# Cross attention and routing of a decoder kernel: another written order, and parts of norms, copies and query scalings exchanged between VectorE and ScalarE

## The chip, the core and the metric

The kernel runs on one core of a Trainium2 chip, which has a tensor engine (TensorE, PE in the profile), a vector engine (VectorE, DVE), a scalar engine (ScalarE, ACT), GpSimd (POOL), and SyncE (SP), whose queue issues most of the DMAs. Each engine works through its own list of instructions in order and waits on semaphores for the others. The metric is the device time of one execution in microseconds.

## The reference

Two decoder layers over x of shape (2, 1024, 256), each step added to x: a linear attention with a feed-forward part, a cross attention to latents, a recurrent cell; then a causal attention, a cross attention to 64 rows of text, and a mixture of experts. The change lies in the last two:

```python
x = x + _L1_attn_ref(_layernorm(x), ...)
x = x + _L1_xattn_ref(_layernorm(x), ctx_768, ...)
x = x + _L1_ffn_ref(_layernorm(x), ...)

# _L1_xattn_ref: 16 heads of 16 channels, 64 keys
q = (x @ wq + bq); k = (y @ wk + bk); v = (y @ wv + bv)
attn = softmax(q k^T / sqrt(16)); out = (attn @ v) @ wo + bo

# _L1_ffn_ref: 8 groups of 256 tokens, 8 experts, room for 64 tokens of a group in each
logits = x @ router_w
dispatch, combine = _gating_top2(softmax(logits), C)   # best two experts, places by running count
hidden = gelu(expert_inputs @ w0) * (expert_inputs @ w1)
expert_outputs = hidden @ wo
```

_layernorm subtracts the mean of a row and divides by the square root of its variance plus 1e-5.

## The kernel before

All 2048 tokens stay in SBUF as `x`, 128 tokens to a tile, 16 tiles. Cross attention and routing go by *units* u = 0 to 3 of four tiles (512 tokens). The class `Cross` has one method for each step of a unit, `Experts` has the routing, and the order of all of it is a text written by hand: `CROSS_ORDER` (L1633), which `Cross.run` reads word by word (L2010). A word names a step, the digit(s) after it the unit and the half, chunk or pair. `FIRST_ORDER` (L2024) does the same for the routing of unit 3 beside the first half of the first expert (L2336). No scheduler moves instructions inside these texts: each engine gets its instructions in this order, and semaphores do the rest.

The steps of a unit in cross attention, with the engine that runs each:

| step | engine | work |
|---|---|---|
| `stat`, `mean` | VectorE | row statistics (L1797), mean and variance (L1803), EPS added (L1804) |
| `root` | POOL | power -1/2 (L144) |
| `norm` | VectorE | (x - mean) x r for two tiles, `ln_apply` (L183) |
| `bias` | POOL | output bias added to x once it is normalised (L204) |
| `turn`, `xT` | TensorE, ScalarE | transposes (L1825), copy from PSUM (L1829) |
| `proj`, `q` | TensorE, both | query projection; + bias and x 0.25: chunk 0 on VectorE (L1846), chunk 1 on ScalarE (L1848) |
| `max`, `red` | TensorE, VectorE | scores once (L1856), row maxima (L1867) |
| `part` | VectorE | the maxima split into three bf16 parts: casts and subtractions (L1878, L1880) |
| `mT`, `rows` | TensorE, ScalarE | maxima transposed (L1890) and copied (L1894) |
| `sc`, `exp` | TensorE, ScalarE | transposed scores minus maxima (L1903), exponentials (L1915) |
| `val`, `os` | TensorE, ScalarE | values (L1922), copy (L1932) |
| `sum`, `inv`, `spr`, `yT` | TensorE, VectorE | sums (L1940), reciprocal (L1949), spread (L1959), product (L1971) |
| `out`, `add` | TensorE, VectorE | output projection (L1979), added to x (L1989) |

`text`, `vals` and `keys` prepare keys and values of a batch entry b (units 0 and 1 use b = 0, units 2 and 3 b = 1). The statistics of units 0 and 1 are taken early, beside the end of the causal attention (`Cross.stats`, L1722).

Routing of unit u is the generator `Experts.scores`, of which each word `route_...` runs the next piece: `stat` (L2126), `mean` (L2130, L2131), `root`, `norm`, `turn` (L2143), `xT` (L2146), `prod` (L2151, the product with the router's weights), `copy` (L2159). `choose` runs one of eight pieces of the top-2 choice of a batch entry, `ones` builds a tile's one-hot places (L2239, L2240), `disp` multiplies tokens by them (L2250, dispatch), `put` copies the result (L2258). `up` is the pair of first products of a chunk of the hidden layer (L2407), eight matmuls of 256 columns in `FIRST_ORDER`; `gelu` (L2418) and `mul` (L2422) follow on ScalarE and VectorE. There are eleven chunks, `00` to `0a`.

PSUM tiles of two banks come from a ring called `s`: three slots in the cross attention stage (`banks("ps_f", 3, 2, 0)`), two with the experts (`banks("ps_c", 2, 2, 2)`). A step that takes a slot waits for the last reader of what lay there.

## Time and profile before

Three runs: 1716.50, 1719.92 and 1722.71 us, median 1719.92. The profile is of one execution more, of 1725.12 us, whose instructions span 1723.4 us.

| stretch, us from the span's start | length | PE busy | DVE busy | ACT busy | POOL busy | granted clock |
|---|---|---|---|---|---|---|
| up to the end of the causal attention, 0 to 1121.6 | 1121.6 | 1064.31 | 612.18 | 412.34 | 216.51 | 0.97 |
| cross attention, routing, start of the experts, 1121.6 to 1268 | 146.4 | 132.72 | 94.81 | 45.75 | 15.54 | 0.92 |
| experts, 1268 to 1723 | 455.0 | 450.55 | 97.03 | 64.42 | 87.55 | 1.00 |

A row of instructions in the profile gives the start and length in us, the engine, the line, the operation, what it writes and reads, and in brackets how long the engine stood idle before it and what it waited for. A length runs from an instruction's start to its end; instructions of one engine that follow one another overlap a little, so four norms of 0.406 us take 1.37 together. In the chain of waits each row is a piece of time on the chain of work that ended last. The granted clock is TensorE's, as a share of its full speed.

### The profile page before, as it was taken

Reading aid. Unit: us, or ns where it says so; the run is one execution under the profiler, and the core shown is the slowest. Engines: PE = TensorE matmul, PEld = TensorE weight load, DVE = VectorE, ACT = ScalarE, POOL = GpSimd, SP = SyncE. Lnnn points to the kernel's source line nnn. Section 1 sums busy time; section 2 is a strip of 40 time slices with the busy share of each in tenths; the row PEclk is TensorE's granted clock in tenths of the full one; section 3 lists DMA queues with packets and bytes.
Section 4 is the critical chain, followed back from the end, with each engine's and each line's share of the span. In section 5 each row is a group of like instructions: output and inputs, shape, how many; then the busy total and the mean of one; then the engine's idle time right before and its main releaser. Section 6 shows DMA issues by size and latency. Waiting matters only on the chain.

```text
span 1723.4 us, 21309 instructions
## 1 busy us (share of the span) xinstructions
PE 1647.6 (96%) x8815; PEld 885.6 (51%) x8822; DVE 804.0 (47%) x1454; ACT 522.5 (30%) x876; POOL 319.6 (19%) x376
## 2 busy tenths in 40 slices
PE   7998899999999999999999999989999999999998
PEld 5746454343433447443433443446785664666466
DVE  8514236646654425476676668376531311111322
ACT  2321231432223323235455455423221111111110
POOL 2001140342222301113111011220035000000520
PEclk9999999999999999979999999989899999999999
DMA  5000000000000100100000000080014322232321
GB/s 232 1 1 3 1 0 0 1 1 1 1 1 1 40 1 1 32 1 2 1 2 1 1 1 1 2 273 2 1 68 164 122 84 66 95 122 72 106 64 49
DMA packets 36824, 69.68 MB, mean 40 GB/s; under 512 B 5048, under 2 KB 28152, under 8 KB 36344
## 3 DMA queue, kind: packets, MB, share of 16 engines
q1 hardware_dynamic: 28712, 53.61, 9.3%
q0 software_dynamic: 4608, 11.54, 2.1%
q10 hardware_dynamic: 3408, 3.17, 0.5%
q8 instruction: 70, 1.15, 0.3%
q14 instruction: 26, 0.21, 0.0%
HBM read 54.15 MB, written 14.16 MB: 40 GB/s over the span
## 4 chain that ended last, share of the span: by engine, by line
PE 80%; DVE 11%; issue 5%; ACT 2%; POOL 1%; DMA 0%; ACTq 0%; POOLq 0%; DVEq 0%
PE ps_s L2407 18%; PE ps_o L2434 9%; PE ps_s L1396 8%; PE ps_o L1436 5%; PE ps_s L1020 4%; PE ps_t L1355 4%; PE ps_o L947 3%; PE ps_t L1201 3%; PE ps_t L1471 2%; PE ps_s L908 2%; PE ps_t L539 2%; PE ps_s L822 2%; PE ps_s L381 2%; DVE part L915 1%; PE ps_f L556 1%
## 5 line engine op out<-in xcount | busy, mean ns | idle before, releaser
L2407 PE MATMUL ps_s<-xe,w 128*128 128x512 f32 (+1 forms) x528 | 229.0, 592 | 0.0
L1506 ACT ACTIVATE pT<-ps_t 128x512 f32<-128x512 f32 (+3 forms) x344 | 150.6, 490 | 150.3 <-PE ps_t L1471 148.9
L1396 PE MATMUL ps_s<-kT,qT 32*128 32x512 f32 (+3 forms) x768 | 182.9, 574 | 10.0 <-DVE part L1412 6.2
L1471 PE MATMUL ps_t<-qT,kT 32*128 32x512 f32 (+3 forms) x688 | 185.6, 557 | 2.2 <-ACT pT L1506 2.2
L2422 DVE TENSOR_TENSOR hid<-ga,ps_s 128x512 f32<-128x512 f32 (+2 forms) x99 | 62.0, 628 | 266.4 <-ACT ga L2418 266.3
L2407 PEld LDWEIGHTS ps_s<-xe,w 128*128 128x128 f32 (+1 forms) x528 | 98.0, 187 | 121.3 <-issue 120.0
L2434 PE MATMUL ps_o<-wo,hid 128*128 128x256 f32 (+1 forms) x704 | 153.7, 379 | 0.0
L1412 DVE TENSOR_REDUCE part<-ps_s 128x2 f32<-128x1024 f32 (+3 forms) x128 | 130.6, 1024 | 46.9 <-PE ps_t L1471 38.8
L2434 PEld LDWEIGHTS ps_o<-wo,hid 128*128 128x128 f32 (+1 forms) x704 | 133.2, 190 | 18.6 <-issue 0.5
L2418 ACT ACTIVATE ga<-ps_s 128x512 f32<-128x512 f32 (+2 forms) x99 | 54.4, 550 | 245.3 <-PE ps_s L2407 244.0
L1464 POOL TENSOR_SCALAR_AFFINE_SELECT pT<-pT 128x256 f32<-128x256 f32 x128 | 52.2, 408 | 319.5 <-ACT pT L1506 311.7
L1396 PEld LDWEIGHTS ps_s<-kT,qT 32*128 32x128 f32 x768 | 61.6, 195 | 86.8 <-issue 45.2
L1436 PE MATMUL ps_o<-pT,vr 128*32 128x256 f32 (+4 forms) x1408 | 99.3, 360 | 1.8 <-POOL pT L1464 1.5
L1027 ACT ACTIVATE pT<-ps_s 128x1024 f32<-128x1024 f32 x64 | 65.5, 1024 | 115.6 <-PE ps_s L1020 115.6
L915 DVE TENSOR_REDUCE part<-ps_s 128x2 f32<-128x1024 f32 x64 | 76.4, 1218 | 28.4 <-PE ps_s L908 27.7
L1032 POOL TENSOR_TENSOR acc<-acc,pT 128x1024 f32<-128x1024 f32 x24 | 59.5, 2480 | 152.7 <-ACT pT L1027 148.1
L1404 DVE TENSOR_TENSOR ps_s<-ps_s,causal 128x256 f32<-128x256 f32 x128 | 55.0, 430 | 66.6 <-PE ps_t L1471 44.6
L2407 PE MATMUL ps_s<-xin,w 128*128 128x256 f32 (+3 forms) x264 | 81.7, 471 | 0.5 <-DVE hid L2422 0.5
L1436 PEld LDWEIGHTS ps_o<-pT,vr 128*32 128x32 f32 x1408 | 29.0, 109 | 99.3 <-issue 85.4
L1471 PEld LDWEIGHTS ps_t<-qT,kT 32*128 32x128 f32 x688 | 71.6, 192 | 12.1 <-ACT pT L1506 6.9
L908 PE MATMUL ps_s<-kT,qT 64*128 64x512 f32 x256 | 71.5, 639 | 0.8 <-DVE part L898 0.6
L1020 PE MATMUL ps_s<-qT,kT 64*128 64x512 f32 x256 | 70.2, 625 | 0.2 <-DVE part L915 0.2
(401 smaller groups left out, 2361.8 us busy)
## 6 DMA issues: line engine op xcount, KB each, us to landing
w<-in_w SPq DMA_DIRECT2D x32, 684.0 KB, 8.5
wo<-in_wo SPq DMA_DIRECT2D x8, 1280.0 KB, 7.0
xi_rows<-xin SPq DMA_DIRECT2D x8, 384.0 KB, 8.1
eo_rows<-rows ACTq DMA_DIRECT2D x12, 256.0 KB, 5.5
xr<-xi_rows POOLq DMA_DIRECT2D x48, 64.0 KB, 7.3
w_ffn<-in_w_ffn SPq DMA_DIRECT2D x1, 2304.0 KB, 13.9
x<-in_x SPq DMA_DIRECT2D x4, 512.0 KB, 5.4
w<-in_w_cell SPq DMA_DIRECT2D x2, 1024.0 KB, 16.5
```

Source lines behind the costliest of these rows:

```text
L908: nc.tensor.matmul(s3[:, hh, :], lhsT=q[rows, qt * P : (qt + 1) * P], rhs=kt[rows, half * 512 : (half + 1) * 512], start=True, stop=True,)
L915: nc.vector.tensor_reduce(part[:, half, qt, :], s3, AX.X, ALU.max, negate=True)
L1020: nc.tensor.matmul(s3[:, hh, :], lhsT=self.ones_h[hr, :] if i else kt[hr, kk * P : (kk + 1) * P], rhs=rows[hr, cols] if i else q[hr, cols] ...
L1027: nc.scalar.activation(pT, s3, AF.Exp)
L1355: nc.tensor.matmul(s, lhsT=self.w[name][:, kc, grp * P : (grp + 1) * P], rhs=self.xT[b][:, kc, cols], start=(kc == 0), stop=(kc == DC - 1),)
L1396: nc.tensor.matmul(s3[:, hh, :n], lhsT=q[rows, qt * P : (qt + 1) * P], rhs=kt[rows, at : at + n], start=True, stop=True,)
L1412: nc.vector.tensor_reduce(out, s3[:, :, :n], AX.X, ALU.max, negate=True)
L1436: nc.tensor.matmul(self.o[hh * 32 : hh * 32 + 32, cols], lhsT=vr[:, kk, 4 * grp + hh, :], rhs=pts[hh // 2][:, hh % 2, cols], start=first, ...
L1471: nc.tensor.matmul(out, lhsT=kt[rows, kk * P : (kk + 1) * P], rhs=q[rows, j * 512 + q0 : (j + 1) * 512], start=True, stop=True,)
L1506: nc.scalar.activation(pT[:, hh, q0:], heads[hh][:, q0:], AF.Exp)
L2407: self.k.nc.tensor.matmul(s[:m, i * 512 : i * 512 + n], lhsT=wt[:, kc, at : at + m], rhs=self.inputs[e][:, kc, first : first + n], start=( ...
L2434: self.k.nc.tensor.matmul(o, lhsT=self.hid[:n, hc, st * P : (st + 1) * P], rhs=self.to[:n, hc, :], start=(hc == 0), stop=(hc == len(HCH) - 1),
```

## The change

A quote mark behind a word of an order (`norm_11'`) now sets `k.other` for that step. Norm steps with it run on ScalarE, as x r + shift with shift = -mean x r, a new small step (`shift`) of each unit on VectorE. Copies with it (`xT`, `rows`, `os`, `route_xT`, `route_copy`, `put`) run on VectorE. `q` with it swaps which engine scales. The words of both orders stand in another sequence: unit 1 goes ahead of unit 0, and the routing, choice and expert steps interleave differently. Six of eight norm steps are marked in the cross attention, six of eight in the routing.

```diff
+    def copy(self, out, in_, act=True):
+        if act != self.other:
+            self.nc.scalar.copy(out, in_)
+        else:
+            self.nc.vector.tensor_copy(out, in_)
...
+    def normed(self, out, in_, mv, r, shift, i):
+        if self.other:
+            self.nc.scalar.activation(
+                out, in_, AF.Identity, bias=shift[:, i : i + 1], scale=r[:, i : i + 1]
+            )
+        else:
+            self.ln_apply(out, in_, mv, r, i)
+
+    def shifted(self, shift, mv, r):
+        self.nc.vector.scalar_tensor_tensor(shift, mv[:, :, 0], -1.0, r, ALU.mult, ALU.mult)
...
 CROSS_ORDER = """
-text_0 stat_31 norm_00 norm_01 stat_30 turn_00 bias_0 turn_01 vals_0 text_1 keys_0 xT_0 stat_20 proj_00
-vals_1 keys_1 proj_01 norm_11 stat_21 q_00 q_01 norm_10 max_01 mean_3 bias_1 mean_2 turn_11 red_010
-turn_10 xT_1 red_011 root_2 proj_11 root_3 norm_21 norm_20 max_00 norm_30 bias_2 norm_31 proj_10 red_001
-bias_3 red_000 q_11 q_10 part_0 max_10 turn_30 red_100 turn_31 xT_3 turn_20 red_101 turn_21 max_11 xT_2
-mT_0 red_110 rows_0 red_111 sc_00 part_1 exp_00 mT_1 rows_1 sc_01 proj_21 exp_01 proj_20 sc_10 q_20 q_21
-val_0 exp_10 max_20 os_0 sum_0 red_200 red_201 sc_11 inv_0 proj_30 exp_11 proj_31 max_21 q_30 q_31 sum_1
-red_210 red_211 spr_0 inv_1 val_1 yT_0 part_2 os_1 out_0 spr_1 add_0 mT_2 route_stat_01 rows_2 yT_1
-route_stat_00 max_30 route_mean_0 route_root_0 out_1 red_300 route_norm_01 route_norm_00 red_301
-route_turn_0 add_1 route_xT_0 route_stat_10 max_31 route_stat_11 red_311 route_prod_0 route_mean_1
-red_310 route_root_1 route_copy_0 route_norm_11 sc_20 route_norm_10 part_3 route_turn_1 exp_20 mT_3
-route_xT_1 sc_21 rows_3 route_prod_1 exp_21 route_copy_1 sc_31 choose_0 choose_0 sum_2 exp_31 choose_0
-choose_0 inv_2 spr_2 choose_0 val_2 choose_0 os_2 yT_2 choose_0 sc_30 choose_0 out_2 exp_30 ones_03
-ones_02 ones_01 ones_00 disp_00 add_2 route_stat_20 sum_3 put_00 ones_07 ones_06 ones_05 val_3 inv_3
-ones_04 spr_3 os_3 route_stat_21 disp_01 yT_3 route_mean_2 put_01 out_3 route_root_2 route_norm_20
-route_norm_21 add_3 route_turn_2 route_xT_2 route_prod_2 route_copy_2
+text_1 norm_10 norm_11' stat_30 norm_01' bias_1 stat_20 turn_11 vals_1 turn_10 keys_1 text_0 xT_1
+norm_00 bias_0 proj_10 vals_0 keys_0 proj_11 stat_21 mean_2 turn_01 root_2 q_11' q_10' turn_00 stat_31
+max_10 xT_0 mean_3 shift_2 root_3 proj_01 norm_20' red_100 norm_21' red_101 proj_00 bias_2 shift_3
+norm_31' max_11 q_00 q_01 norm_30' turn_20 red_110 turn_21 bias_3 xT_2 red_111 turn_31 turn_30 part_1
+max_00 xT_3 red_000 mT_1 rows_1 red_001 max_01 red_010 red_011 sc_11 part_0 exp_11 mT_0 rows_0 sc_10
+proj_20 exp_10 proj_21 sc_00 q_21 q_20 val_1 exp_00 max_20 os_1' sum_1 red_200 red_201 sc_01 inv_1
+proj_31 exp_01 proj_30 max_21 q_31' q_30' sum_0 red_210 red_211 spr_1 inv_0 val_0 yT_1 part_2 os_0 spr_0
+out_1 yT_0 mT_2 add_1 max_31 rows_2 route_stat_11 out_0 route_stat_10 route_mean_1 red_311 route_root_1
+route_shift_1 red_310 route_norm_10' route_norm_11' add_0 sc_21 route_stat_01 route_turn_1 exp_21
+route_stat_00 route_mean_0 route_xT_1' route_root_0 max_30 route_shift_0 route_norm_00' route_prod_1
+red_301 route_norm_01' red_300 route_turn_0 part_3 sc_20 route_xT_0 route_copy_1' mT_3 exp_20
+route_prod_0 rows_3' sc_30 route_copy_0 choose_0 sum_2 exp_30 val_2 inv_2 choose_0 choose_0 spr_2 os_2
+choose_0 yT_2 choose_0 choose_0 sc_31 choose_0 out_2 exp_31 choose_0 ones_03 ones_01 ones_02 sum_3 add_2
+route_stat_20 val_3 inv_3 ones_00 route_stat_21 spr_3 os_3 route_mean_2 disp_00 yT_3 route_root_2
+route_shift_2 route_norm_21 route_norm_20' out_3 ones_06 put_00 ones_07 ones_05 ones_04 route_turn_2
+add_3 disp_01 route_xT_2 route_prod_2 put_01 route_copy_2
 """
...
 FIRST_ORDER = """
-up_06 route_stat_30 up_08 gelu_06 route_stat_31 route_mean_3 mul_06 route_root_3 gelu_08 mul_08 up_04
-route_norm_30 route_norm_31 route_turn_3 gelu_04 mul_04 route_xT_3 route_prod_3 up_01 route_copy_3
-choose_1 choose_1 choose_1 gelu_01 choose_1 up_00 choose_1 mul_01 choose_1 gelu_00 mul_00 up_0a choose_1
-choose_1 up_05 gelu_0a ones_12 ones_13 up_07 gelu_05 ones_10 ones_11 mul_0a gelu_07 disp_10 mul_07
-mul_05 up_02 put_10 ones_15 ones_16 ones_14 up_09 gelu_02 ones_17 mul_02 disp_11 gelu_09 mul_09 up_03
-put_11 gelu_03 mul_03
+route_stat_30 route_stat_31 route_mean_3 route_root_3 route_shift_3 up_09 route_norm_30 route_norm_31'
+route_turn_3 gelu_09 up_07 route_xT_3' mul_09 route_prod_3 gelu_07 mul_07 up_0a route_copy_3' choose_1
+choose_1 up_06 gelu_0a choose_1 choose_1 choose_1 gelu_06 mul_0a mul_06 up_08 choose_1 choose_1 up_03
+gelu_08 mul_08 choose_1 up_02 gelu_03 ones_13 ones_10 up_01 ones_11 gelu_02 ones_12 mul_03 disp_10
+gelu_01 mul_02 mul_01 up_04 put_10 ones_15 ones_16 ones_14 up_05 gelu_04 ones_17 mul_04 disp_11 gelu_05
+mul_05 up_00 put_11' gelu_00 mul_00
 """
...
+    def shift(self, u):
+        mv, r, sh = self.early[u]
+        self.k.shifted(sh, mv, r)
...
-        if c == 0:
-            k.nc.vector.tensor_scalar(q[:, 0, :], s[:, :512], k.vec("xq_b", 0), 0.25, ALU.add, ALU.mult)
+        s = s[:, c * 512 : (c + 1) * 512]
+        if (c == 0) != k.other:
+            k.nc.vector.tensor_scalar(q[:, c, :], s, k.vec("xq_b", c), 0.25, ALU.add, ALU.mult)
         else:
-            k.nc.scalar.activation(q[:, 1, :], s[:, 512:], AF.Identity, bias=self.qb[:, 1:2], scale=0.25)
+            k.nc.scalar.activation(q[:, c, :], s, AF.Identity, bias=self.qb[:, c : c + 1], scale=0.25)
...
         for step in CROSS_ORDER.split():
-            name, args = step.rsplit("_", 1)
+            k.other = step.endswith("'")
+            name, args = step.rstrip("'").rsplit("_", 1)
```

## The prediction

> **What bounds the kernel now.** I read the page's busy shares and slices first, then the busy time by stage, then the chain of waits inside the stage that the change rewrites, then single instructions there.

> ```profile
> PE 1647.6 (96%) x8815; PEld 885.6 (51%) x8822; DVE 804.0 (47%) x1454; ACT 522.5 (30%) x876; POOL 319.6 (19%) x376
> PE   7998899999999999999999999989999999999998
> PEclk9999999999999999979999999989899999999999
> ...
> 1121.60:1268.00 146.40, 132.72 (x1202) 93.62 (x1201) 94.81 (x254) 45.75 (x63) 15.54 (x10) 0.92 0.25 81
> 1268.00:1723.00 455.00, 450.55 (x1506) 277.08 (x1504) 97.03 (x191) 64.42 (x112) 87.55 (x112) 1.00 0.30 96
> ```

> The first number after each stretch is its length, the next is TensorE's busy time, and the one before the DMA share is the granted clock. TensorE bounds the whole (96%), and nearly all of what comes after 1268 us (450.55 of 455.00). The rewritten stage is 1121.6 to 1268 us: 13.7 us without a matmul (146.40 - 132.72), and a clock of 0.92. Only these two can be won, since the number of matmuls doesn't change.

> ```profile
> 1130.00:1140.00 10.00, 6.71 (x46) 3.86 (x44) 9.93 (x25) 1.70 (x2) 5.20 (x4) 0.69 1.01 386
> 1140.00:1150.00 10.00, 8.07 (x118) 5.40 (x116) 8.88 (x13) 2.58 (x3) 3.94 (x2) 0.97 0.92 244
> ...
> 1190.00:1200.00 10.00, 8.52 (x83) 5.63 (x85) 8.01 (x21) 5.04 (x6) 1.01 (x1) 0.93 0.01 2
> ...
> 1230.00:1240.00 10.00, 8.90 (x37) 7.53 (x35) 4.89 (x19) 2.87 (x4) 1.01 (x1) 0.66 0.01 2
> ```

> Where TensorE waits most, VectorE (third pair of numbers) is full: 9.93 of 10 us, while ScalarE works 1.70. The chain of waits runs almost wholly over VectorE from 1122.0 to 1147.9 us, and again from 1182.0 to 1198.3. Part of it, and the same time on POOL:

> ```profile
> 1132.91 2.13 DVE ve L1804
> 1135.67 2.01 POOL rs_y L144 x2
> 1137.70 4.70 DVE xh L183 x8
> 1142.40 2.27 DVE m L1867 x2
> ...
> 1132.66 2.35 POOL L204 TENSOR_TENSOR x<-x,rows 128x1024 f32<-128x1024 f32 x1 [5.39 <-DVE xh L183]
> 1139.15 2.45 POOL L204 TENSOR_TENSOR x<-x,rows 128x1024 f32<-128x1024 f32 x1 [1.48 <-DVE xh L183]
> ```

> The add of EPS to 128x4 numbers (L1804) takes 2.13 us here and 0.17 us the next time; eight norms take 4.70 us where four take 1.37. Both overrun while a bias add runs on POOL, and end as it ends: 4.0 us lost (2.13 - 0.17, and 4.70 - 8 x 0.34).

> **The change, part by part.** Durations below are pitches where instructions follow one another: a norm 0.345 us on VectorE (1.37 / 4), 0.50 on ScalarE (the three norms of L1311 at 671.9 us take 1.58, one alone 0.59), a statistics pair 0.66, keys 1.41, values 0.46, one max reduction 1.135, the three-way split `part` 1.5.

> *Up to the end of the second split (before: 1122.46 to 1154.25 us, 31.8).* VectorE's work is memset 0.48, eight statistics 2.65, sixteen norms 5.5, values 0.92, keys 2.82, means 1.05, two query scalings 1.4, eight reductions 9.1, two splits 3.0: 26.9, with 4.0 blocked and 0.9 waiting. Six of the eight norm steps are primed and leave VectorE (12 x 0.345 = -4.1); two `shift` come (+0.3). ScalarE takes them in idle time (12 x 0.5 = 6.0 in a stretch where it works 1 to 3 us in 10). The query scalings only swap sides: whichever comes second waits for the first, as before (the ScalarE one starts at 1131.97, when VectorE's ends). The blocked 4.0 go: placing the steps in their new order at these pitches, bias_1 runs 1123.8 to 1126.2 and bias_0 1127.6 to 1130.0, beside statistics, keys and values, which ran at normal pace beside a bias add before (1124.9 to 1127.3), and bias_2 lies beside work that reads PSUM. But bias_3 now waits for the late norm_30' on ScalarE (about 1139.4) and runs to 1141.9, over part_1, due at 1140.3. Before, both splits ran after the last bias add. What that costs the rows don't show: nothing, or all 1.6 us. [...] By the row alone (only single-input norms and the EPS add were seen blocked) it may be 0[...]. I take 1.6. Waits for TensorE: 1.0 for q_00 behind two projections, 1.2 for max_10 and max_11. End: 1122.46 + 26.9 - 4.1 + 0.3 + 1.6 + 2.2 = 1149.4, 4.8 earlier.

> From there to the end of max_20 TensorE took 11.7 us before (to 1165.92). Now mT 0.6, scores 1.3, proj 3.6, scores 1.3, val 1.9 with a 0.2 wait, max 1.1 = 10.0. That would be 6.4 us gained; but 1.5 of it is full clock where the rows of before are slow (mT 1.01 and scores 2.41 at 1154), and TensorE again stands about 2 us ahead of mT_0, so I take the same slow rows: **-5.0** (between -6.4 and -1.5, the latter if the projections of unit 0 also run at half clock: 8 x 0.43 = 3.4 on q_00's path).

> *Second stretch (1177.07 to 1204.93).* From yT to the end of part_3 VectorE loses eight norms (-2.76), gains the copy xT_1 (a PSUM copy of that size is 1.22 on VectorE, L444, 1.01 on ScalarE) and two shifts (+0.24): -1.3, with 0.2 less waiting, -1.5. Behind part_3 lay mT_3, scores, route product, scores (6.66, two of them slow); now one score step stands ahead of mT_3 and 4.6 remain: -2.1. os_1 and rows_3 as VectorE copies (1.22, and 0.69 after the bf16 copy L935) fall where VectorE waited 2 to 6 us. Sum -3.5; less 0.8 for half clock, which low activity may bring here as before (0.93): **-2.7** (-3.5 to -0.5).

> *Third stretch, to the end of route product 2 (1204.93 to 1234.32).* The matmuls alone are 25.5. Before, TensorE waited 1.07 for the copy os_2 and 1.10 for xT_2, and the product ran 2.67 instead of 2.05. Now val_2 stands ahead of the choose steps (1.8 us of TensorE work over a 1.01 copy), and disp_01 (1.8) between turn_2 and product 2: **-2.8** (-3.5 to -1). If the cover were gone, the two copies would be back at 2.2.

> *First expert half (1234.32 to 1267.45, 33.1).* Group 3's statistics can't begin before product 2 ends, since they reuse the closed pool's memory (VectorE waited 3.48 for it before). Chain: statistics 1.4, mean 0.9, root 1.0, shift and hand-overs 0.5, ScalarE's norms 1.1 = 4.7 us. Before, three ups (24 matmuls) covered it; now one does, at 1.78: TensorE idles 2.9. Then up_07 is a third user of two PSUM slots: up_09 holds one until mul_09, turn_3 the other until xT_3', both queued on VectorE, mul_09 behind the copy (and gelu_09 behind norm_31' and a 1.28 table load): 1.5 more. Behind up_07 wait product 3 and the choice, and the scatter behind that. After such idling I expect half clock for about 3.4 us. [...] while the row 1230:1240 shows 0.66 after waits of 1.1. [...] by the row 3.5, 1.4, 2.7. I take the row. Sum: 1.8 + 2.9 + 1.4 + 1.5 + 3.5 + 2.7, then eight ups 14.2, choice 1.8, dispatch 3.6, small waits 0.6 = 34.0: **+0.9** (-1.7 to +3).

> *Without effect:* two shifts in the attention before (0.17 each where VectorE idles 2 to 7 us); put_11', copy_1', copy_3' (under 0.5 each, beside ups). No moved step issues a DMA and SP's queue keeps its order; POOL only gets its bias adds and roots at other times. After 1268 us TensorE is full and everything moves up as one.

> **Sum.** -5.0 - 2.7 - 2.8 + 0.9 = -9.6. The profiled execution: span 1723.4 to 1713.8, its time 1725.1 to 1715.5. The median before, 1719.9, is 5.2 below that execution; the same step gives 1710.3.

> **Rivals.** (1) *The clock eats the gain.* Each microsecond of matmuls at half clock costs 0.5. If the first stretch (-1.5), the second (-0.5) and the expert start (+1) come near their bad ends and the third holds: -3.8, so 1716.1. For it: 0.69, 0.93 and 0.66 all follow short waits. Against: turn_01 and turn_00 now fill the gap ahead of max_10. (2) *Everything fits:* full clock after mT_0 and in the expert start, part_1 not blocked: 1.5 + 1.6 + 0.8 + 2.5 more, 1704. Against: four bad ends must all fail. (3) *Slower:* the expert start stays at half clock. One up costs 1.78 more; the gain of 10.5 up to there is used up after six ups, and if all eight later ups and the dispatches run so, (14.2 + 3.6) - 10.5 + 0.9 = +8, 1728. For it: 1230 to 1250 us had about 10 us at half clock. Against: in a run of ups the clock was back at 1.00 by 1250. (4) *The gain is given back later,* where weights arrive for the experts: those of the first two are in by 1150, later loads follow the slots they reuse, and TensorE waits 4.5 us in 455, so this only adds to (1).

> **How the numbers follow.** My forecast has 0.62 (1705.5 to 1715), rival 1 with 4 has 0.20, rival 2 has 0.12, rival 3 has 0.06. 0.3% of this time is 5.2 us, about what a measurement can tell from no change: the bounds are 1714.7 and 1725.1. Faster: 0.58 + 0.12 + 0.05 = 0.75; same 0.04 + 0.15 = 0.19; slower 0.06. The range reaches from rival 2, less 1, to the near side of no change: 1703 to 1718.5.

> **What would show it.** L1804 at 0.17 us and no run of norms above its pitch; part_1's first cast near 1.9 us under bias_3; the second split ending near 1149.4; max_20 ending near 1161, the fourth score step near 1197, product 2 near 1224, the second dispatch of the first half near 1258. TensorE's waits of 2.9 and 1.5 us around turn_3, the second for xT_3' or mul_09. Wrong would be: VectorE no longer full up to the second split with ScalarE's norms late instead; a clock under 0.9 over 1121 to 1260; or a step of before that I held fixed moving by itself.

## The result, and the profile after

The changed kernel took 1719.64 us (median of 12 runs, 1707.97 to 1723.59). The kernel before, timed again beside it, took 1724.45 (12 runs, 1716.50 to 1726.71). The medians lie 4.8 us apart. The ratio on record is 0.9963, 95% interval 0.9945 to 0.9982, which makes it 6.4 us. Two later comparisons gave 0.9964 (0.9945 to 0.9983; e8) and 0.9964 (0.9948 to 0.9981; e15), again with medians only 4.9 and 4.6 apart, so the gain is known as some 5 to 6 us. The forecast was 1710.3 with a range of 1703 to 1718.5, so the direction was right and the size wrong: 9.6 us were forecast, and 1719.64 lies above the range.

The profiled execution of the changed kernel took 1708.17 us with a span of 1706.4. That is 17.0 us less than the profiled execution before, and most of it has nothing to do with the change. The last add of the layer before, which ends the unchanged part, starts at 1121.99 us before and at 1111.34 after (one row of each profile):

```profile
1121.99 0.42 DVE L1549 TENSOR_TENSOR x<-x,ps_t 128x256 f32<-128x256 f32 x1 [1.45 <-PE ps_t L1544]
1111.34 0.42 DVE L1569 TENSOR_TENSOR x<-x,ps_t 128x256 f32<-128x256 f32 x1 [1.44 <-PE ps_t L1564]
```

These 10.65 us lie in code that is the same in both but for two shift steps of 0.16 us. The stretch view shows where some of it comes from (columns as in the prediction; the clock is the third number from the end). Before, then after:

```profile
720.00:760.00 40.00, 35.53 (x181) 16.12 (x179) 26.51 (x40) 9.58 (x21) 3.68 (x9) 0.62 0.00 1
150.00:200.00 50.00, 39.37 (x121) 22.61 (x120) 24.37 (x72) 12.58 (x22) 12.54 (x20) 0.90 0.00 0
```

```profile
720.00:760.00 40.00, 36.10 (x252) 16.46 (x254) 30.73 (x44) 12.63 (x33) 6.25 (x16) 0.79 0.00 1
150.00:200.00 50.00, 39.36 (x135) 22.01 (x134) 24.77 (x72) 14.04 (x24) 12.19 (x17) 1.00 0.00 1
```

The granted clock differs in equal code, 0.62 against 0.79. A later profile of the changed kernel (e15) has the 0.62 and 0.90 of before, and its last add at 1122.04. So the clock's course differed between executions of one kernel (0.79 and 0.62 over the same 40 us), and the two profiles may be compared only inside the stage, with times counted from that last add. The page after, and the stage with what follows:

```profile
PE 1631.9 (96%) x8815; PEld 879.0 (52%) x8822; DVE 801.7 (47%) x1446; ACT 529.2 (31%) x892; POOL 319.3 (19%) x376
...
PEclk9999999999999999989999999999899999999999
```

```profile
1111.10:1249.50 138.40, 127.13 (x1194) 91.42 (x1194) 91.24 (x242) 51.73 (x78) 15.50 (x10) 0.94 0.26 85
1249.50:1706.00 456.50, 452.00 (x1513) 278.39 (x1511) 97.86 (x193) 64.26 (x111) 87.36 (x112) 1.00 0.30 96
```

The stage takes 138.4 us where it took 146.4; of these 8.0, 0.87 are four output products that lay in the stage before and lie behind it now (the rest is 456.5 against 455.0 us). VectorE is busy 3.6 us less and ScalarE 6.0 more, as the marks say.

Two details of the first stretch. VectorE and POOL in the timeline:

```profile
1124.04 2.35 POOL L224 TENSOR_TENSOR x<-x,rows 128x1024 f32<-128x1024 f32 x1 [1.43 <-ACT xh L198]
1124.63 1.78 DVE L205 SCALAR_TENSOR_TENSOR sh<-mv,rs_y 128x4 f32<-128x4 f32 x1
1129.23 2.36 POOL L224 TENSOR_TENSOR x<-x,rows 128x1024 f32<-128x1024 f32 x1 [2.84 <-ACT xh L198]
1129.48 2.29 DVE L1905 CAST mparts<-m 128x64 bf16<-128x64 f32 x1
```

bias_3 covers part_1, and its first cast takes 2.29 us where the next take 0.32: the blocked split of the prediction, at about its price (1.9 there). What the prediction did not have is shift_3 (L205) under bias_2, 1.78 us for 128x4 numbers; shift_2 takes 0.15. Both end as the bias add does: the cast at 1131.77 us beside 1131.59, shift_3 at 1126.41 beside 1126.39. The add of EPS (L1827 now), 2.13 us before, is short both times:

```profile
1119.54 0.17 DVE L1827 TENSOR_SCALAR ve<-mv 128x4 f32<-128x4 f32 x1
1121.34 0.17 DVE L1827 TENSOR_SCALAR ve<-mv 128x4 f32<-128x4 f32 x1
```

Then the expert start, TensorE's timeline and two stretches of it. Product 3 is the route product of unit 3 (L2183). A row's `x` counts what the trace records, two to each f32 matmul of the program that is no transpose (product 3 is a loop of eight and has `x16`, the eight transposes ahead of it have `x8`), so an up's `x8` are four matmuls there.

```profile
1216.33 1.48 PE L2175 MATMUL ps_s<-ident,w 128*128 128x128 f32 x8 [2.10 <-DVE w L191]
1219.25 3.78 PE L2441 MATMUL ps_s<-xin,w 128*128 128x256 f32 x8 [1.44 <-DVE xT L133]
1222.82 3.42 PE L2183 MATMUL ps_t<-router,xT 128*128 128x8 f32 x16
1226.09 6.50 PE L2441 MATMUL ps_s<-xin,w 128*88 128x256 f32 x16
```

```profile
1220.00:1224.00 4.00, 4.00 (x15) 3.37 (x13) 0.42 (x1) 0.92 (x2) 0.00 (x0) 0.50 0.00 0
1224.00:1228.00 4.00, 4.00 (x16) 3.37 (x17) 1.45 (x7) 1.71 (x3) 0.00 (x0) 0.50 0.00 0
```

The two waits are there, 2.10 and 1.44 us for the 2.9 and 1.5 forecast. But half clock lasts from about 1218 to 1232, over most of the second wait, up_07, product 3 and most of two more ups: 13.65 us where I allowed 3.4.

### The profile page after: what moved, and what is told of

Same layout as the page of the kernel before. It is cut to its first block, busy times and chain, and to the rows that moved or that the text cites. A ratio compares the mean times of both kernels' runs of the same rounds, so it can differ in the third digit from the quotient of the medians.

```text
span 1706.4 us, 21317 instructions
## 1 busy us (share of the span) xinstructions
PE 1631.9 (96%) x8815; PEld 879.0 (52%) x8822; DVE 801.7 (47%) x1446; ACT 529.2 (31%) x892; POOL 319.3 (19%) x376
## 2 busy tenths in 40 slices
PE   7998899999999999999999999989999999999998
## 5 line engine op out<-in xcount | busy, mean ns | idle before, releaser
L1416 PE MATMUL ps_s<-kT,qT 32*128 32x512 f32 (+3 forms) x768 | 177.8, 551 | 11.0 <-DVE part L1432 7.1
L2456 DVE TENSOR_TENSOR hid<-ga,ps_s 128x512 f32<-128x512 f32 (+3 forms) x99 | 62.1, 628 | 268.4 <-ACT ga L2452 268.3
L1491 PE MATMUL ps_t<-qT,kT 32*128 32x512 f32 (+3 forms) x688 | 181.7, 545 | 2.2 <-ACT pT L1526 2.2
L2468 PEld LDWEIGHTS ps_o<-wo,hid 128*128 128x128 f32 (+1 forms) x704 | 133.3, 190 | 18.5 <-issue 0.5
L2452 ACT ACTIVATE ga<-ps_s 128x512 f32<-128x512 f32 (+3 forms) x99 | 54.4, 549 | 254.2 <-PE ps_s L2441 254.2
L935 DVE TENSOR_REDUCE part<-ps_s 128x2 f32<-128x1024 f32 x64 | 76.4, 1219 | 28.3 <-PE ps_s L928 27.7
L967 PE MATMUL ps_o<-pT,vr 128*64 128x512 f32 x256 | 69.9, 627 | 0.9
## 6 DMA issues: line engine op xcount, KB each, us to landing
w_ffn<-in_w_ffn SPq DMA_DIRECT2D x1, 2304.0 KB, 14.2
```

The costliest lines, as they stand in the source:

```text
L935: nc.vector.tensor_reduce(part[:, half, qt, :], s3, AX.X, ALU.max, negate=True)
L967: nc.tensor.matmul(self.o[hh * 64 : hh * 64 + 64, :], lhsT=self.vr[b][:, kk, h * 64 : (h + 1) * 64], rhs=pT[:, hh, :], start=first, stop=last,
L1416: nc.tensor.matmul(s3[:, hh, :n], lhsT=q[rows, qt * P : (qt + 1) * P], rhs=kt[rows, at : at + n], start=True, stop=True,)
L1491: nc.tensor.matmul(out, lhsT=kt[rows, kk * P : (kk + 1) * P], rhs=q[rows, j * 512 + q0 : (j + 1) * 512], start=True, stop=True,)
L2456: self.k.nc.vector.tensor_mul(self.hid[:m, hc, first : first + n], self.act.pop(hc)[:m, :n], self.now.pop(hc)[:m, 512 : 512 + n])
L2468: self.k.nc.tensor.matmul(o, lhsT=self.hid[:n, hc, st * P : (st + 1) * P], rhs=self.to[:n, hc, :], start=(hc == 0), stop=(hc == len(HCH) - 1),
```

## The experiments

Each experiment was compared with runs of the kernel before on its own chip. On the chips used after the first group (e1, e2, e6, e7), every kernel takes about 26 us more, behind the stage, where TensorE waits (in e15 it is busy 80.82 us of the first 100 after the stage, in the first profile after 100.00), so only ratios can be compared between chips. Times "in the stage" count from the last add; product 2 is the route product of unit 2. *Windows* is the time lost to half clock from the last add to the end of the second dispatch of the first expert half, the sum of (1 - granted clock) over 2 us slices, divided by 1.71 us. It came out within 0.03 of a whole number in all 19 profiles. In the first profiles before and after, the stretches at a granted clock of 0.50 last 3.413 us or 2, 3, 4 or 7 times that (but for one that the end of the span cuts off), so they are counted in windows of 3.41 us, each of which loses half of that; a run of windows without a break is called a spell. *Net* is the length less that loss, so roughly what the written order is worth by itself (an estimate: a window that falls into a wait is counted in full).

| profile | product 2 ends | second dispatch ends | windows | net | ratio to before, 95% interval |
|---|---|---|---|---|---|
| before | 112.3 | 145.5 | 7 | 133.5 | |
| before again (e16) | 115.4 | 148.7 | 9 | 133.3 | |
| changed | 101.1 | 138.2 | 5 | 129.6 | 0.9963 (0.9945 to 0.9982) |
| changed (e8) | 101.0 | 138.2 | 5 | 129.7 | 0.9964 (0.9945 to 0.9983) |
| changed (e11) | 107.9 | 140.2 | 7 | 128.3 | |
| changed (e15) | 107.9 | 143.5 | 9 | 128.1 | 0.9964 (0.9948 to 0.9981) |
| e1 old expert order | 107.8 | 142.1 | 9 | 126.8 | 0.9972 (0.9949 to 0.9994) |
| e2 new expert order alone | 111.8 | 143.1 | 6 | 132.9 | 0.9976 (0.9959 to 0.9992) |
| e3 order without marks | 108.0 | 139.7 | 5 | 131.1 | 0.9954 (0.9931 to 0.9977) |
| e4 marks without order | 115.3 | 148.5 | 9 | 133.1 | 1.0001 (0.9981 to 1.0022) |
| e5 earlier bias | 105.1 | 142.2 | 9 | 126.8 | 0.9978 (0.9952 to 1.0004) |
| e6, e14 earlier bias, old expert order | 105.0 | 134.4, 134.3 | 5 | 125.9, 125.8 | 0.9935 (0.9917 to 0.9954), 0.9920 (0.9897 to 0.9943) |
| e7, e12 warm waits | 101.0, 107.9 | 133.6, 140.4 | 1, 6 | 131.9, 130.2 | 0.9954 (0.9933 to 0.9974) |
| e9 expert marks gone | 107.9 | 139.5 | 7 | 127.6 | 0.9941 (0.9920 to 0.9963) |
| e10 e9 and earlier bias | 97.6 | 129.2 | 1 | 127.5 | 0.9941 (0.9918 to 0.9964) |
| e13 dense products | 106.0 | 139.5 | 4 | 132.6 | 0.9959 (0.9933 to 0.9986) |
| e17 e14 with dense products | 104.5 | 138.8 | 5 | 130.2 | 0.9916 (0.9889 to 0.9942) |

Profiles with the old expert order (before, e1, e4, e6, e14, e16, e17) have the 0.87 us of output products inside.

**The expert order undone, and alone (e1, e2).** e1 is the changed kernel with the old text of the expert start (and the new shift step in it), e2 the old cross attention text with the new expert start.

```diff
 FIRST_ORDER (e1)
-route_stat_30 route_stat_31 route_mean_3 route_root_3 route_shift_3 up_09 route_norm_30 route_norm_31'
-route_turn_3 gelu_09 up_07 route_xT_3' mul_09 route_prod_3 gelu_07 mul_07 up_0a route_copy_3' choose_1
...
+up_06 route_stat_30 up_08 gelu_06 route_stat_31 route_mean_3 mul_06 route_root_3 route_shift_3 gelu_08
+mul_08 up_04 route_norm_30 route_norm_31 route_turn_3 gelu_04 mul_04 route_xT_3 route_prod_3 up_01
...
 CROSS_ORDER (e2)
-text_1 norm_10 norm_11' stat_30 norm_01' bias_1 stat_20 turn_11 vals_1 turn_10 keys_1 text_0 xT_1
...
+text_0 stat_31 norm_00 norm_01 stat_30 turn_00 bias_0 turn_01 vals_0 text_1 keys_0 xT_0 stat_20 proj_00
...
```

> The new kernel with the old order of the first expert half (route_shift_3 added, no marks there). Stage = from the start of the last add of causal attention to the end of the second dispatch of the first expert half: 145.5 us before, 138.2 in the new kernel. Theory (the new first half costs 4.8 us, four of them half clock after two uncovered waits): the stretch from the end of route product 2 to that dispatch goes back from 37.1 to about 33 us including four output matmuls (0.9), the stage to about 134, and the time to 0.994 of before. Rival (the half clock there comes by chance or from the transposes and thin router products, whatever the order): that stretch stays near 37 and the stage near 138.

> The old order of cross attention, all unmarked, with the new order and marks of the first expert half. Theory: the stage is 4 to 5 us longer than before (149 to 150 us), the time 1.002 to 1.003 of before. Rival (the loss came from where the new cross order leaves the clock): within 1 us of 145.5.

Medians 1720.29 and 1721.30 us beside 1724.37. Both expectations missed: e1's way from product 2 to the second dispatch is 34.3 us (about 33 expected), but its stage is 142.1 and not 134; and e2 is not slower than before but faster (143.1 us, 0.9976). In e1's profile the cross attention came out 6.8 us longer than in the changed kernel's, although both run the same instructions up to product 2: a spell of half clock lies over 70 to 83 us there (the expectations below say 68 to 83), and none does in the first profile after. So one profile was not enough to price the expert order. Net, e1 is at 125.9 without the output products and the changed kernel at 128.1 to 129.7: the new expert start costs 2.2 to 3.8 us there. Behind the old cross attention it costs 0.2 to 0.4 (132.9 in e2, 132.5 and 132.6 before without the output products). In the times no cost shows (0.9972 against 0.9963, and e2 below 1), so they can't be read as the worth of the order alone: e2 has six windows in its profile where the kernel before has seven and nine.

**The changed kernel again (e8, e11, e15).**

> The changed kernel once more, for a second profile and for its spread. Its first profiled execution (1708.2 us, mean clock 0.987) had one spell of about 14 us at half clock in this stage, over up_07 and product 3, while the kernel with the old expert order (e1) ran the same instructions up to product 2 with such a spell 68 to 83 us after the last add of the layer before. Theory: where a spell falls is not tied to the two waits around turn_3 but to how the clock happens to run in an execution; a profile with a mean clock of 0.974 to 0.981 shows the spell at 68 to 83 us, product 2 ending near 107.8 (not 101.1) and the way from there to the second dispatch near 34 (not 37.1). Rival: the two waits cause the spell; product 2 ends near 101 again and the way on is 37 again. Median 1719 to 1721 by both.

> The changed kernel, a third profile. Theory: the way from product 2 to the second dispatch is 37 us again, with waits of 2.1 and 1.4 us and four windows at half clock, however the clock ran ahead of the stage; the stretch up to product 2 is 101 us, or 108 if a spell falls 68 to 83 us after the last add. Rival (chance): the way is 32 to 34.

> The changed kernel beside it: ratio 0.9963, the stage 138.2 or 140.2 us by pattern.

My theory of pure chance fell with e8: the same spell over the expert start, 37.1 us from product 2 to the second dispatch. The rival, that the two waits cause a spell of that length, fell with e11: the waits are again 2.10 and 1.44 us, one window follows, and that way takes 32.3 us; in e15, 35.7 with three (a third pattern; 138.2 or 140.2 us were expected). e11's TensorE at the expert start, where product 3 now runs at full clock:

```profile
1236.66 3.38 PE L2441 MATMUL ps_s<-xin,w 128*128 128x256 f32 x8 [1.44 <-DVE xT L133]
1239.87 1.85 PE L2183 MATMUL ps_t<-router,xT 128*128 128x8 f32 x16
```

In e11 and e15 a spell of four windows lies at 70 to 83 us as well. So it is neither a free scatter nor fixed: the spells come back at the same two places, and which of them, and for how many windows, differs between executions. What decides it is worked out below, at the end of this section.

**Is it idleness? (e7, e12)** Useless matmuls of 256 columns, into a tile that nothing reads, fill the two waits.

```diff
-route_shift_3 up_09 route_norm_30 route_norm_31' route_turn_3 gelu_09 up_07
+route_shift_3 up_09 warm_8 route_norm_30 route_norm_31' route_turn_3 gelu_09 warm_6 up_07
```

> The new kernel with 8 and 6 matmuls of 128x256 without use put into the two waits around turn_3 (their result goes to a spare PSUM tile that nobody reads). Theory that TensorE's idleness halves the clock: up_07, product 3, up_0a and up_06 run at full clock (8 matmuls in 2.0 us instead of 3.8), the stretch gets 5 to 7 us shorter than 37.1. Rival (transposes and thin products halve it, or the waits are too short to matter): they still take 3.8 us, and the stretch stays at 37 or grows by up to 1.5.

> The kernel e7 again (8 and 6 useless matmuls of 256 columns in the two waits), a second profile. Theory: no half clock between product 2 and the second dispatch, the way 32.4 us as in e7. Rival (chance): a spell somewhere in it, 35 to 39 us.

No half clock comes over the expert start in either, and it takes 32.6 us from product 2 to the second dispatch in both. That is 4.5 us less than the changed kernel with four windows there, and nothing less than e11 with one. Over all executions it didn't pay measurably (0.9954, against 0.9963 without).

**What starts the spell at 70 us (e13).** TensorE in e15 over that time, and the stretches:

```profile
1186.74 1.09 PE L2175 MATMUL ps_s<-ident,w 128*128 128x128 f32 x8
...
1188.65 1.16 PE L1883 MATMUL ps_s<-keys,q 32*128 32x128 f32 x28 [0.40 <-ACT pT L1942]
1189.74 1.95 PE L2183 MATMUL ps_t<-router,xT 128*128 128x8 f32 x16
1191.55 1.75 PE L2175 MATMUL ps_s<-ident,w 128*128 128x128 f32 x8
...
1197.66 3.52 PE L2183 MATMUL ps_t<-router,xT 128*128 128x8 f32 x16
```

```profile
1185.04:1189.04 4.00, 3.60 (x36) 2.15 (x40) 3.93 (x12) 3.29 (x5) 0.49 (x1) 1.00 0.00 0
1189.04:1193.04 4.00, 4.00 (x48) 3.66 (x44) 3.80 (x7) 2.07 (x4) 0.52 (x1) 0.84 0.02 4
1193.04:1197.04 4.00, 4.00 (x17) 1.37 (x16) 0.79 (x4) 1.45 (x2) 0.00 (x0) 0.50 0.00 0
```

TensorE is busy 3.60 and 4.00 of 4 us, with a single wait of 0.40, and the clock halves all the same. What stands there are score products on 32 rows (`32*128`) and a route product of eight columns (`128x8`): busy, with little work in each instruction. e13 leaves the waits as they are and puts six useless matmuls of 256 columns ahead of route products 1 and 0, into the PSUM tile that the product then overwrites.

```diff
         t = k.t()
+        for _ in range(6 if u < 2 else 0):
+            nc.tensor.matmul(t[:, :D], lhsT=k.ident, rhs=xT[:, 0, :D], start=True, stop=True)
```

> The changed kernel with six useless matmuls of 256 columns ahead of route products 1 and 0 (1.3 us each at full clock). Theory: the spell at 68 to 83 us follows stretches in which TensorE is busy but with little in each instruction (32-row score products, products of eight columns), so it is missing now: in an execution with a clock of 0.75, 0.82, 0.60 over 20 to 32 us after the last add, product 2 ends near 103.6 to 104 (107.8 without the extra matmuls) and the median is 3 to 4 us under the changed kernel's, in spite of 2.6 us of useless work. Rival: the spell comes by the clock's own course or after waits; product 2 ends near 110 in such an execution and the median is 2 to 3 us over the changed kernel's.

> The kernel before, a second profile. Theory: like the changed kernel it has two patterns; if the clock ahead of the stage runs the same as in the first profile (last add near 1122 us) the stage is 145.5 us again to within 0.3, otherwise its half-clock windows fall elsewhere and it is 140 to 148. Rival: its stage is always 145.5.

e13's profile has the same clock as e11 and e15 up to there (0.74, 0.83, 0.59 over 20 to 32 us). Its half-clock windows start at 21.92 and 28.75 us in the stage, theirs at 21.95 to 21.96 and 28.78 to 28.79, so the windows fall on the same instructions; e1, e9 and e12 are alike up to there too, and all five have the spell. e13 has none of it (columns as above):

```profile
1185.28:1189.28 4.00, 3.60 (x36) 2.14 (x40) 3.93 (x12) 3.28 (x5) 0.50 (x1) 1.00 0.00 0
1189.28:1193.28 4.00, 4.00 (x43) 3.57 (x39) 3.79 (x7) 2.07 (x4) 0.51 (x1) 1.00 0.02 4
1193.28:1197.28 4.00, 4.00 (x41) 2.97 (x41) 0.98 (x4) 1.48 (x2) 0.00 (x0) 1.00 0.00 0
```

TensorE is as busy and waits the same 0.40 us, but the instructions are other ones, and so is the clock. At this place, then, the clock went with the work in the instructions (0.50 in e15, 1.00 in e13) and not with the waits (0.40 us in both); e17 below has 1.00 there where e14 has 0.50. At the expert start e13 has two windows of half clock (111 to 117 us). Product 2 ends 1.9 us earlier than in e11 and e15, at 106.0 (103.6 to 104 expected, reckoned without the 1 us of half clock before 32 us); the median is 1.9 under the changed kernel's beside it, less than can be told, where 3 to 4 were expected. The kernel before (e16) has patterns too, 145.5 and 148.7 us, at the same net of 133.3 to 133.5; but its last add was near 1122 us both times, so my expectation that the clock ahead fixes the pattern was wrong.

**Order alone and exchange alone (e3, e4).** e3 takes all marks off both new texts; e4 sets the marks on the old texts. Of each, one line:

```diff
 e3
-norm_31' max_11 q_00 q_01 norm_30' turn_20 red_110 turn_21 bias_3 xT_2 red_111 turn_31 turn_30 part_1
+norm_31 max_11 q_00 q_01 norm_30 turn_20 red_110 turn_21 bias_3 xT_2 red_111 turn_31 turn_30 part_1
...
 e4
-turn_10 xT_1 red_011 root_2 proj_11 root_3 norm_21 norm_20 max_00 norm_30 bias_2 norm_31 proj_10 red_001
+turn_10 xT_1 red_011 root_2 proj_11 root_3 shift_2 shift_3 norm_21' norm_20' max_00 norm_30' bias_2 norm_31' proj_10 red_001
...
```

> The changed kernel without its marks: both new orders, but norms, copies and query scalings on the engines of before. Theory (the marks take 12 norms off a full VectorE): second split ends near 31.5 us after the last add of the layer before (27.9 with the marks, 32.2 before), the score and route steps behind it keep their shorter path, and 3 to 4 us of the change's 4.4 are gone: median about 1722.5. Rival: the order alone is the gain, as it takes the two blocked stretches away; second split near 28.5, median about 1720.

> The orders of before with the marks and the shift steps: the exchange alone. Theory: VectorE is relieved of 4.1 less 0.3 us up to the second split, but the two blocked stretches of before (4.0 us lost) are there still in part: second split near 29 us (32.2 before), second stretch 1 us shorter, median about 1721. Rival: without the new order ScalarE's norms only end later than VectorE's and nothing moves: 32 us, median 1724.4 as before.

e3 is as fast as the whole change (0.9954 against 0.9964 on the same chip), e4 as slow as before (1.0001). The second split ends at 30.45 us in e3, 27.85 in e8: the marks do shorten VectorE's first stretch by 2.6 us, and net e3 stands 1.5 to 3 us behind. But in the times no part of the gain can be put down to the marks. In e4 the second split ends at 32.70 us, no earlier than before (32.21): as the rival said, nothing moves there. VectorE, with fewer norms, waits 4.9 us for score products in that stretch, where it waited 1.2 before.

**The blocked split and shift (e5, e6, e14).** shift_3, norm_31' and norm_30' go ahead of the reductions, and bias_3 runs before part_1. e5 keeps the new expert start, e6 and e14 are one kernel with the old one.

```diff
-norm_20' red_100 norm_21' red_101 proj_00 bias_2 shift_3
-norm_31' max_11 q_00 q_01 norm_30' turn_20 red_110 turn_21 bias_3 xT_2 red_111
+norm_20' norm_21' shift_3 red_100 red_101 proj_00 bias_2
+norm_31' norm_30' bias_3 max_11 q_00 q_01 turn_20 red_110 turn_21 xT_2 red_111
```

> The changed kernel with shift_3, norm_31', norm_30' and with them bias_3 moved ahead of bias_2's end, so that bias_3 no longer lies over part_1 and shift_3 not under bias_2; the new expert order stays. Theory: second split 1.9 us earlier (25.95 us as in e6, 27.86 without), median 1.9 under the changed kernel's, about 1718; the rest of what e6 won (6.4 against e1 with the same bias edit) was a half-clock spell that the old expert order didn't have there. Rival: the early bias takes the spell away itself and brings all 6 us: median about 1714.

> The new kernel with the old first expert half and, in the cross attention, shift_3 ahead of red_100 and norm_31', norm_30' and bias_3 ahead of max_11, so that no bias add lies beside shift_3 (1.78 us there) or part_1's cast (2.29). If VectorE's blocked time is on the path, the second split ends 1.9 us earlier than in the new kernel (26.0 instead of 27.9 us after the start of the stage), the stage about 132, the time 0.993 of before. Rival (TensorE's max steps bound it): the split moves by less than 0.5 us and the stage is that of the old first half alone, about 134.

> The kernel e6 again (new cross attention order with the earlier bias, old expert order), beside the changed kernel on the same chip. Theory: ratio to before 0.9935 again and 4 to 6 us under the changed kernel; the stage up to the second dispatch 134 to 136 us. Rival: e6's six executions were luck; 0.996 as the changed kernel.

The second split ends at 25.95 to 25.97 us in all three, 1.9 before the changed kernel's 27.85. That is what the two blocked instructions cost on the path, of the 3.6 us that they last longer than unblocked (1.78 less 0.15, 2.29 less 0.32). e5 nevertheless gained nothing that can be told (0.9978, median 1749.20 beside e8's 1746.04 on that chip): its profile has nine windows. e14 ran beside e15 on one chip: 1739.53 against 1746.64 us, ratios 0.9920 and 0.9964 with intervals that don't overlap. It beats both kernels. Its expert start, TensorE's timeline:

```profile
1226.36 3.70 PE L2441 MATMUL ps_s<-xin,w 128*128 128x256 f32 x16
1230.78 1.99 PE L2441 MATMUL ps_s<-xin,w 128*128 128x256 f32 x8 [0.72 <-DVE hid L2456]
1232.61 1.04 PE L2175 MATMUL ps_s<-ident,w 128*128 128x128 f32 x8
1234.84 1.92 PE L2183 MATMUL ps_t<-router,xT 128*128 128x8 f32 x16 [1.19 <-ACT xT L131]
```

Three ups ahead of the transposes cover most of the statistics of unit 3: waits of 0.72 and 1.19 us in place of 2.10 and 1.44, and a clock of 1.00 to the second dispatch in both e6 and e14 (e1, with the same expert start, had three windows there).

**The marks of the expert start (e9, e10), and both cures (e17).** e9 is the changed kernel without the four marks of the expert text; e10 adds the earlier bias; e17 is e14 with e13's matmuls.

```diff
-route_stat_30 route_stat_31 route_mean_3 route_root_3 route_shift_3 up_09 route_norm_30 route_norm_31'
-route_turn_3 gelu_09 up_07 route_xT_3' mul_09 route_prod_3 gelu_07 mul_07 up_0a route_copy_3' choose_1
+route_stat_30 route_stat_31 route_mean_3 route_root_3 route_shift_3 up_09 route_norm_30 route_norm_31
+route_turn_3 gelu_09 up_07 route_xT_3 mul_09 route_prod_3 gelu_07 mul_07 up_0a route_copy_3 choose_1
...
```

> The changed kernel with the four marks of the expert order gone (norm_31, xT_3, copy_3, put_11), its new sequence kept. Theory: norm_31' on ScalarE puts gelu_09 and its table load 1.1 us back, and xT_3' stands ahead of mul_09 on VectorE, so up_07 waits 1.44 us behind turn_3; without the marks mul_09 frees the slot early, up_07 waits 0.28 (as in the profile of the kernel without any marks), the half-clock spell is one window of about 3.4 us in place of four, and the way from product 2 to the second dispatch is about 31.7 us (37.1 with the marks). Ratio to the kernel before about 0.9935. Rival: the spell comes by chance; the way stays at 37 or varies, ratio 0.996 as with the marks.

> The same with shift_3, norm_31', norm_30' and bias_3 of the cross attention moved earlier too. Theory: second split at 25.95 us after the last add (27.86 in the changed kernel), expert way 31.7; if the two add up, 0.9925 or about 3.5 us under the kernel with only the marks gone or 13 us under the kernel before. Rival: the early bias only moves the half-clock spell to 68 to 80 us, as in the two profiles with it, and the ratio is that of e9 or worse.

> The kernel e14 (earlier bias, old expert order) with e13's six useless matmuls of 256 columns ahead of route products 1 and 0. Theory: its long spell over the route products (three windows, some 5.1 us lost) is missing, 2.6 us of useless work come in: the stage up to the second dispatch is about 132 us (134.3 in e14) and the ratio to before 0.9905 to 0.992. Rival: the clock halves somewhere later in place of it, as at the expert start in e13: 135 us or more, ratio 0.993 or above.

e9's TensorE:

```profile
1234.80 1.64 PE L2175 MATMUL ps_s<-ident,w 128*128 128x128 f32 x8 [2.10 <-DVE w L191]
1236.73 3.38 PE L2441 MATMUL ps_s<-xin,w 128*128 128x256 f32 x8 [0.28 <-DVE hid L2456]
```

The second wait falls from 1.44 to 0.28 us as expected: on ScalarE xT_3 no longer stands ahead of mul_09, which frees the slot. The way to the second dispatch is 31.6 us with one window, also as expected. But against e11, with the same clock up to there and the marks, only 0.7 us are left at the second dispatch, and the window count is seven in both; that the marks by themselves bring four windows is refuted. The ratio 0.9941 hit the number, and its interval also holds 0.9963. e10's profile, with one window, is the shortest of all (129.2); its ratio is e9's, so the earlier bias added nothing measurable there. In e17 the spell of three windows over the route products is gone, and three come at the expert start instead, which ran at full clock in e14. The same two places in e14, then in e17:

```profile
1191.12:1201.36 10.24, 10.24 (x60) 6.09 (x60) 2.42 (x10) 2.99 (x5) 0.00 (x0) 0.50 0.00 0
1235.69:1245.93 10.24, 10.24 (x61) 9.05 (x61) 7.38 (x35) 4.52 (x8) 0.00 (x0) 1.00 0.00 0
```

```profile
1189.48:1199.72 10.24, 10.24 (x107) 8.02 (x110) 2.70 (x10) 3.75 (x5) 0.00 (x0) 1.00 0.00 0
1234.05:1244.29 10.24, 10.24 (x34) 8.80 (x34) 3.69 (x17) 3.39 (x5) 0.00 (x0) 0.50 0.00 0
```

That is the rival's course in the profile (138.8 us), while the ratio, 0.9916, fits the theory and can't be told from e14's.

**How many windows: the work in each (all traces).** The traces hold the start and length of every half-clock stretch. In each of the 19 profiles the stretches of the stage start at whole multiples of 3.413 us from one another, to within 0.04 us: in the first profile before 6, 19, 29 and 33 times 3.413 us after the first of them, in that of the changed kernel 23, in e15 2, 14 and 27. In the two first profiles this holds over the whole span. So the work of each window of such a grid can be counted and set beside the clock of the next. The count is an estimate, from the shapes and times of the recorded matmuls with weights of my choice: an f32 record of 256 columns in the largest form of the rows (`128*128`) counts 1, a bf16 record half; others count by their columns and by their share of the `128*128`; one that crosses a border is split by time. A window full of whole f32 matmuls comes to about 15.8 so, at half clock to half of that. Over the 19 traces (9314 windows, from 20 to 1700 us):

| work in a window | windows | of these, the next at half clock |
|---|---|---|
| under 5.5 | 408 | 400 |
| 5.5 to 6.2 | 101 | 75 |
| above 6.2 | 8805 | 0 |

A single cut at 6.1 tells the next window's clock wrongly in 29 of the 9314, the best cut on TensorE's busy time in 310. In 104 of the 475 half-clock windows the window ahead was busy throughout. At the two places (the start of a window in the stage, then TensorE's busy us and the work in it):

| profile | route products: start, busy, work | next clock | expert start: start, work of this window and those that follow until the clock is back |
|---|---|---|---|
| changed | 65.9, 3.41, 6.3 | full | 103.4: 4.0, then at half clock 4.9, 3.4, 3.7, 7.2 |
| e11 | 66.3, 3.13, 4.5 | half | 110.7: 4.0, then at half clock 6.1 |
| e15 | 66.3, 3.12, 4.5 | half | 110.7: 4.0, then at half clock 6.0, 2.4, 4.4 |
| e13 | 66.3, 3.10, 12.0 | full | 107.3: 3.8, then at half clock 3.8, 6.8 |

So in each of these half clock starts behind the waits: the window with most of the first wait and the transposes is busy 1.4 us and does 4.0 or less. In these rows half clock then lasted until a window at half clock had about 6 again, and that went with which instructions fell into one window: 6.1 in e11 was just enough and 6.0 in e15 just not. (The count is not finer than about 0.1: in e11's other spell a window of 6.1 was not enough. e15's last, 4.4, is one of the 29; it holds the chunk of 88 columns, which would come to 6.4 if it counted as 128.) At the route products the instructions of the first profile lie 0.55 us earlier in their window than e11's, and it holds 6.3 instead of 4.5. This count was made after the runs and no run was made to test it, but in e7, e12, e13 and e17 matmuls put into such a window took the half clock behind it away.

## Why the prediction was wrong

Against the first profile before, counted from the last add:

| step of the prediction | forecast | changed | e15 |
|---|---|---|---|
| to the end of max_20 | -5.0 | -4.4 | -3.4 |
| to the fourth score step | -2.7 | -2.9 | +2.0 |
| to the end of route product 2 | -2.8 | -4.0 | -3.1 |
| first expert half | +0.9 | +4.0 | +2.5 |
| sum | -9.6 | -7.3 | -2.0 |

The like-for-like numbers of the last step are 0.87 higher, for the output products.

That the first three steps add up to -11.3 in the first profile, beside -10.5 forecast, is luck in part: e15, the same kernel, has -4.5.

*First stretch.* The prices were right: the add of EPS back to 0.17 us, part_1 blocked under bias_3. The 0.6 that were missing in the first profile are less than shift_3's 1.78 us under bias_2, for which I had not allowed ("two `shift` come (+0.3)"). The 1.6 for part_1 was an estimate of mine: the rows of before show no cast beside a bias add. The same estimate for shift_3 would have found this.

*Second and third.* Sound to about 1.2 us where the clock stayed up. The -2.7 contained 0.8 for half clock; the changed kernel's first two profiles have none there, e11 and e15 have four windows, 6.8 us.

*Expert half: the step that failed.* "After such idling I expect half clock for about 3.4 us" put the length at one window. That was an estimate of mine; the first profile before has 3.41 us of half clock in the stage three times (from 1154.19, 1198.56 and 1246.35 us) and 6.83 twice (from 1133.71 and 1232.70). The start was right: waits of 2.10 and 1.44 us (2.9 and 1.5 forecast, where the chain given as 4.7 adds up to 4.9), and half clock behind them in all four profiles of the changed kernel. The length was wrong: four, four, one and three windows, so 6.8, 6.8, 1.7 and 5.1 us lost, and the step came to +4.0 in the first profile instead of +0.9. What the prediction put at nothing is the work within the instructions behind the waits. Half clock went on until a window held about 6, and the windows with the second wait, up_07, product 3, whose records have eight columns, and the start of a chunk of 88 columns held 4.9, 3.4 and 3.7; product 3 took 3.42 us at half clock, not 2.7. Where one window came (e11), the step is -0.8, or +0.1 like for like, no worse than forecast. On whether half clock starts, the row 1230:1240 (0.66), from which I took 3.5, 1.4 and 2.7 us for up_07, turn_3 and product 3, was right. Rival 1, "the clock eats the gain" at -3.8, named the cause; it had only 0.20. Measured, the gain was 4.8 by the medians and 6.4 by the ratio.

*The sum.* Net of the clock the stage went from 133.4 (132.5 without the output products) to 128.1 to 129.7: 2.8 to 4.4 us. The rest of the gain lies in the windows, seven and nine in two profiles before, five, five, seven and nine in four after. By mean length, 147.1 less 0.87 to 140.0, the stage won 6.2 us, beside 4.8 to 6.4 in the times; six profiles of few patterns make that a fair agreement and no proof. *The anchor:* the median of three runs shown was 1719.92, twelve gave 1724.45. 1719.64 lies 9.3 above 1710.3: 4.5 from this, 4.8 from the smaller gain between the medians. The note that the profiled execution stood 5.2 above the median was correct, and it was the median that was low: 42 later runs on one chip spread from 1710.53 to 1729.00 around 1724.37.

What stays open: why the grid and the instructions stand to each other as they do in a given execution, and which part of the new cross attention order holds its gain; only the whole text was tried.

## What to carry to other kernels

Before pricing a stage, count its half-clock windows and set the net lengths side by side; take several profiles of either kernel, since one pair here showed 17.0 us where some 5 to 6 were real. Look for half clock under instructions with few rows or columns as well as behind waits, and try dense products between them: six matmuls of 256 columns ahead of each of two route products took the clock there from 0.50 (e15) to 1.00 (e13), though no gain in the times could be told from the changed kernel's (0.9959 against 0.9964). What the clock went with here was the estimated work in each 3.41 us: no half clock after more than 6.2 (8805 windows), and 400 times of 408 after less than 5.5. A step moved to another engine is worth its time only on the path: the marks took 2.6 us off VectorE's first stretch, and the order alone was as fast as far as can be told (0.9954 against 0.9964).
